# Cross-attention on one core: the third token group's softmax moves its subtraction and its row sums into ScalarE's exponentials

## The chip, the core and the metric

The kernel runs on one core of one Trainium2 chip. The time is the device time of one execution in microseconds (us), the median over the runs shown. A core has five engines that run side by side, each with its own in-order queue: TensorE (PE in the profile; its weight loads are PEld), VectorE (DVE), ScalarE (ACT), GpSimd (POOL) and SyncE (SP, which here only issues transfers). They wait for each other through semaphores.

## What is computed

A cross-attention layer with residual. 2 batches of 2048 tokens with 640 channels ask 154 context rows of 1024 channels; there are 20 heads of 32 channels. The context is cut in two halves of 77 rows, "text" and "ip", with key and value weights of their own, and each half has a softmax of its own; the two results are added.

```python
q = split_heads(hidden_states @ Wq.T)
k, v = split_heads(text @ Wk.T), split_heads(text @ Wv.T)
k_ip, v_ip = split_heads(ip @ Wk_ip.T), split_heads(ip @ Wv_ip.T)
def attend(q, k, v):
    scores = einsum('bhsd,bhld->bhsl', q, k) / sqrt(32)
    return einsum('bhsl,bhld->bhsd', softmax(scores, axis=-1), v)
out = merge_heads(attend(q, k, v)) + merge_heads(attend(q, k_ip, v_ip))
return out @ Wo.T + bo + hidden_states
```

The softmax takes each row's maximum away before the exponential, and divides by the row's sum. Everything is in fp32.

## The kernel before, in words

**Units.** The work is cut into 20 units. A unit is one batch, one chunk of 128 channels (4 heads) and one block of 1024 tokens. The 128 tokens that stand on the partitions at a time are a tile, so a unit has 8 tiles; they are taken in three groups, `GROUPS = ((0, 3), (3, 3), (6, 2))`: groups 0 and 1 have three tiles each, group 2 (the "third group") two. A tile has 4 heads x 2 halves = 8 softmax rows of 77 per partition, so groups 0 and 1 have 24 rows (1848 elements) per partition and group 2 has 16 rows (1232 elements).

**The steps of one group**, each a word in a schedule, with the unit's number behind the dot and the group's number in front of it (E2.5 is step E of group 2 in unit 5):

- R (`scores`, L223): TensorE computes the scores of the group into four PSUM banks, one per head.
- K (`take`, L235): ScalarE copies the four banks into the buffer `pb` in SBUF, one copy per bank. Only then may TensorE use these banks again.
- M (`maxima`, L261): VectorE takes the maximum of each row.
- S (`subtract`, L275): GpSimd subtracts it, in place.
- E (`exponential`, L281): ScalarE takes the exponential of the whole group in one instruction, in place.
- D (`sums`, L288 and L290): VectorE sums each row, and takes the reciprocal.
- N (`normalise`, L295): GpSimd multiplies by it.
- T (`transpose`, L302): VectorE transposes 32 x 32 blocks in place.

After two units comes A (`attend`, L311): TensorE multiplies the transposed weights with the values, and CA (`take_attention`, L334 and L338) copies the result out on ScalarE. Beside this stand, per chunk, the projections of keys and values (k and v, L132; ck and cv are their copies on ScalarE, L673 and L675), the query projections (q, L191; cq is the scaled copy on ScalarE, L201), and, from unit 10 on, the output projection of the first batch (words m, o, cm, co and G; L457 to L508), written as seven products in place of eight. The output projection of the second batch comes last, after the last attend (words V, X, F, Y; L815 to L835).

**What sets the order.** The list `SCHEDULE` is written out by hand, and `emit` turns each word into instructions in that order. Each engine's queue follows the order of its own words. For ScalarE the words are K, E, cq, ck, cv and CA; for VectorE M, D, T and the sums of the output projection; for GpSimd S, N and G. Two halves of four PSUM banks serve everything on TensorE: "@0" and "@1" behind an R or an A name the half, "@4" behind a q or a k the single bank. So a K, cq, cv, ck or CA that is late on ScalarE holds a bank (or the queries) that TensorE needs for a later word.

The change touches `exponential_of` (L244, which the kernel before never calls, since `DIRECT` is empty), `maxima` (L257), `sums` (L285), `normalise` (L293) and the dispatch in `emit` (L650 to L663). The schedule itself stays as it is.

Of the kernel before, what the change touches and what calls it, by code (L numbers as in the profile page):

```python
# [20 lines left out]
def kernel(  # L21
# [25 lines left out]
    nc = tc.nc  # L47
    P = 128
    NC = C // P
    NCC = CC // P  # L50
    G = P // D
# [7 lines left out]
    L = TEXT  # L59
# [1 line left out]
    NK = (2 * L + D - 1) // D  # L61
    LP = NK * D
    SCALE = 1.0 / float(D) ** 0.5
    DIRECT = {}
    NP = B * NC
    NU = NP * SUB
    OPEN = 4
# [4 lines left out]
    small = ctx.enter_context(tc.tile_pool(name="small", bufs=4))  # L72
# [137 lines left out]
    def keys_of(u, s):  # L210
        return pb_of(u, s)[:, :, :, : 2 * L]

    def rows_of(u, s):
        return keys_of(u, s).rearrange("p n g (t l) -> p (n g) t l", l=L)

    def scores(u, s, ps):

        _, b, c, _ = step_of(u)
        first, n = GROUPS[s]
        for t in range(n):  # L220
            h, st = divmod(first + t, TB // P)
            for g in range(G):
                nc.tensor.matmul(  # L223
                    ps[g][:, ts(t, 2 * L)],
                    qTs[(u, h)][g * D : (g + 1) * D, ts(st, P)],
                    kT[g * D : (g + 1) * D, c, b].rearrange("p t l -> p (t l)"),
                    start=True,
                    stop=True,
                )

    def take(u, s, ps):

        n = GROUPS[s][1]
        for g in range(G):
            nc.scalar.copy(  # L235
                keys_of(u, s)[:, :, g], ps[g][:, : n * 2 * L].rearrange("p (n l) -> p n l", n=n)
            )
# [3 lines left out]
    def rows_in(ps, n):  # L241
        return ps[:, : n * 2 * L].rearrange("p (n t l) -> p n t l", n=n, t=2)

    def exponential_of(u, s, ps):  # L244

        n = GROUPS[s][1]
        for g in range(G):
            for t in range(n):
                for x in range(2):
                    nc.scalar.activation(  # L250
                        rows_of(u, s)[:, t * G + g, x],
                        rows_in(ps[g], n)[:, t, x],
                        AF.Exp,
                        bias=maxs[(u, s)][:, t * G + g, x : x + 1],
                    )

    def maxima(u, s, ps=None):  # L257
        n = GROUPS[s][1] * G
        mx = small.tile([P, n, 2], F32, tag=f"mx{n}", name=f"mx_{u}_{s}")
        if ps is None:  # L260
            nc.vector.tensor_reduce(mx, rows_of(u, s), AX.X, ALU.max)  # L261
# [21 lines left out]
    rdens = {}  # L283

    def sums(u, s):  # L285
        n = GROUPS[s][1] * G
        den = small.tile([P, n, 2], F32, tag=f"den{n}", name=f"den_{u}_{s}")
        nc.vector.tensor_reduce(den, rows_of(u, s), AX.X, ALU.add)  # L288
        rden = small.tile([P, n, 2], F32, tag=f"rden{n}", name=f"rden_{u}_{s}")
        nc.vector.reciprocal(rden, den)  # L290
        rdens[(u, s)] = rden

    def normalise(u, s):  # L293
        n = GROUPS[s][1] * G
        nc.gpsimd.tensor_tensor(  # L295
            rows_of(u, s), rows_of(u, s), rdens[(u, s)].unsqueeze(3).to_broadcast([P, n, 2, L]), ALU.mult
        )

    def transpose(u, s):
# [4 lines left out]
    def attend(q, pa):  # L304

        zones = pb[:, ds(q % 2, SUB)].rearrange("p z n g (k s) -> p (z n) g k s", k=NK)
        for k in range(NK):
            for r in range(G):
                rows = slice(r * D, (r + 1) * D)
                for g in range(G):  # L310
                    nc.tensor.matmul(  # L311
                        pa[r][g * D : (g + 1) * D, :],
                        v4s[q % 2][rows, g, k, :],
                        zones[rows, :, g, k, :],
                        start=(k == 0),
                        stop=(k == NK - 1),
                    )
# [10 lines left out]
    def take_attention(q, pa):  # L328
        b, c = divmod(q, NC)
        rows = rows_of_attention(b, c).rearrange("p i (n r s) -> p r i n s", n=NT // NH, r=G)  # L330
        for r in range(G):
            tokens = pa[r].rearrange("p (i n s) -> p i n s", i=NHB, n=NT // NH)
            if q % 2 == 0:
                nc.scalar.copy(rows[:, r], tokens)  # L334
                continue

            for sub in range(SUB):
                nc.scalar.copy(rows[:, r, ts(sub, NH)], tokens[:, ts(1 - sub, NH)])  # L338
# [204 lines left out]
    for t in range(2):  # L543

        ps = halves[t][G - 2 + t]
# [76 lines left out]
    def emit(word):  # L622
        name, _, where = word.partition("@")
        k, *args = name.split(".")
        x, y = (*(int(a) for a in args if a.isdigit()), None, None)[:2]
        i = int(k[1:]) if k[1:].isdigit() else None
        if k[0] == "R":
            at[name] = halves[int(where)]
            scores(x, i, at[name])
        elif k == "A":  # L630
            at[name] = halves[int(where)]
            attend(x, at[name])
        elif k == "CA":
            take_attention(x, at[f"A.{x}"])
        elif k == "SQ":
            square_v(x)
        elif k == "VS":
            spread_v(x, y)
        elif k == "LX":
            load_block(x, y)  # L640
        elif k == "LQ":
            load_wq(x)
        elif k == "LK":
            load_w(x)
        elif k == "LO":
            load_wo()
        elif k == "LF":
            for part in PARTS:
                fetch(0, part)
        elif k[0] in "KMSEDNT":  # L650
            ps = at[f"R{i}.{x}"]
            if k[0] == "K":
                take(x, i, ps)
            elif k[0] in "ME":
                direct = (x, i) in DIRECT
                if k[0] == "M":
                    maxima(x, i, ps if direct else None)
                elif direct:
                    exponential_of(x, i, ps)
                else:  # L660
                    exponential(x, i)
            else:
                dict(S=subtract, D=sums, N=normalise, T=transpose)[k[0]](x, i)  # L663
        elif k == "q":
            at[name] = banks[int(where)]
            queries(x, y, at[name])
        elif k == "cq":
            take_queries(x, y, at[name[1:]])
        elif k in ("k", "v"):
            at[name] = banks[int(where)]  # L670
            project_kv(4 * x + 2 * (k == "v") + y, at[name])
        elif k == "ck":
            nc.scalar.copy(kT[:, x, :, y, :], keys_in(at[name[1:]]))  # L673
        elif k == "cv":
            nc.scalar.copy(vT[:, :, ds(y * L, L)], keys_in(at[name[1:]]))  # L675
        elif k in ("o", "p"):
            at[name] = banks[int(where)]
            last_chunk(at[name], int(k == "p"), x, range(NC - (k == "p")))
        elif k == "co":
            store_last(at[name[1:]], 0, x)  # L680
        elif k[0] == "m":
            at[name] = banks[int(where)] if where else at[f"m{JOINS[i]}.{x}"]
            product(i, 0, x, at[name])
        elif k[:2] == "cm":
            take_product(int(k[2:]), 0, x, at[name[1:]])
        elif k[0] == "W":
            sum_w(i)
        elif k[0] == "G":
            sum_t(i, 0, x)
        else:  # L690
            finish(k, args, where)
# [152 lines left out]
    for word in SCHEDULE:  # L844
        emit(word)
# [32 lines left out]
```

## Time and profile before

| | |
|---|---|
| median of 2 runs | 509.73 us (509.55 to 509.91) |
| the profiled execution: first to last instruction (span) | 509.3 us, mean granted TensorE clock 0.990 |
| busy of TensorE / VectorE / GpSimd / ScalarE | 496.4 / 431.5 / 414.3 / 242.8 us |
| chain that ended last, by engine | PE 69%, DVE 9%, DMA 8%, POOL 8%, ACT 2% |

How to read it. A group's row gives the line, the engine and the operation, the tiles written and read, the shape, the count, then the busy time, the mean duration of one in ns, and the idle time of the engine in front of these instructions with what ended it ("<-POOL pb L275" means: a result of line 275 on GpSimd). In a timeline the first two columns are the start and the length in us; instructions of one kind that follow each other are merged ("x4"). The busy time of TensorE counts pipelined matmuls by modelled ends, so the gaps between starts say more than the busy share. The clock in the table is the share of the TensorE clock that was granted.

### The profile page before, as it was taken

What the parts mean: (1) busy time and instruction counts of PE and PEld (TensorE: products, weight loads), DVE (VectorE), ACT (ScalarE), POOL (GpSimd) and SP (SyncE); (2) the same over time, 40 slices, a digit from 0 to 9 for tenths busy, and PEclk for the clock granted to TensorE, in tenths of its full rate; (3) what the DMA queues carried; (4) which work ended last, traced back from release to release, by engine and by line L of the source; (5) the groups of instructions that cost most, each with busy time, mean ns of one, the idle gap of its engine ahead of it and who ended that gap; (6) DMA issues with size and microseconds to landing.
All of it is one profiled execution on the core that took longest, in us unless ns stands there. A gap on an engine that the chain in (4) does not pass through costs nothing.

```text
span 509.3 us, 9862 instructions
## 1 busy us (share of the span) xinstructions
PE 496.4 (97%) x4114; PEld 292.1 (57%) x4114; DVE 431.5 (85%) x401; ACT 242.8 (48%) x423; POOL 414.3 (81%) x176
## 2 busy tenths in 40 slices
PE   9999999999989999999999999996999999999996
PEld 5657557557458556446655565553666576444442
DVE  0078989989987989977995999799299999999986
ACT  1266657577566567654636544663466453100000
POOL 0078999999997979988998899799399999468750
PEclk9999999999999999999999999997999999999999
DMA  8994050502441554577444724534914022310017
GB/s 272 357 287 134 16 136 11 142 3 71 129 148 42 157 192 141 200 238 250 146 134 146 242 62 155 210 106 134 322 30 124 27 82 64 125 62 1 21 62 268
DMA packets 67468, 69.34 MB, mean 136 GB/s; under 512 B 5472, under 2 KB 47200, under 8 KB 67424
## 3 DMA queue, kind: packets, MB, share of 16 engines
q1 hardware_dynamic: 66704, 68.00, 42.5%
q8 instruction: 32, 0.52, 0.4%
q10 hardware_dynamic: 720, 0.72, 0.4%
q14 instruction: 12, 0.10, 0.1%
HBM read 54.94 MB, written 10.49 MB: 128 GB/s over the span
## 4 chain that ended last, share of the span: by engine, by line
PE 69%; DVE 9%; DMA 8%; POOL 8%; ACT 2%; SPq 2%; issue 1%; DVEq 0%; POOLq 0%
PE bank L191 22%; PE bank L835 11%; PE bank L477 8%; PE bank L223 8%; PE bank L311 6%; PE bank L132 6%; POOL pb L275 5%; PE bank L457 4%; DMA x<-in_x_dram 3%; DVE pb L302 3%; POOL pb L295 3%; PE bank L487 2%; DVE mx L261 2%; DVE den L288 2%; DMA wo_ct<-in_L_xattn_Wo_dram 2%; DMA aT<-in_L_xattn_Wk_ip_dram 2%
## 5 line engine op out<-in xcount | busy, mean ns | idle before, releaser
L275 POOL TENSOR_TENSOR pb<-pb,mx 128x1848 f32<-128x1848 f32 (+1 forms) x60 | 175.6, 2946 | 42.4 <-DVE mx L261 42.3
L295 POOL TENSOR_TENSOR pb<-pb,rden 128x1848 f32<-128x1848 f32 (+1 forms) x60 | 175.6, 2948 | 15.4 <-DVE rden L290 15.1
L191 PE MATMUL bank<-x,wq 128*128 128x512 f32 x400 | 182.5, 606 | 4.8 <-DMA x<-in_x_dram 4.5
L261 DVE TENSOR_REDUCE mx<-pb 128x24 f32<-128x1848 f32 (+1 forms) x60 | 109.3, 1837 | 34.4 <-ACT pb L235 34.4
L191 PEld LDWEIGHTS bank<-x,wq 128*128 128x128 f32 x400 | 75.0, 193 | 92.8 <-issue 82.8
L235 ACT COPY pb<-bank 128x462 f32<-128x462 f32 (+1 forms) x240 | 101.9, 534 | 54.2 <-PE bank L223 53.6
L281 ACT ACTIVATE pb<-pb 128x1848 f32<-128x1848 f32 (+1 forms) x60 | 94.9, 1583 | 68.0 <-POOL pb L275 67.8
L288 DVE TENSOR_REDUCE den<-pb 128x24 f32<-128x1848 f32 (+1 forms) x60 | 110.2, 1836 | 16.3 <-ACT pb L281 16.3
L302 DVE STREAM_TRANSPOSE pb<-pb 128x1920 f32<-128x1920 f32 (+1 forms) x60 | 114.6, 1924 | 0.9 <-POOL pb L295 0.9
L223 PEld LDWEIGHTS bank<-kT,qT 32*128 32x128 f32 x1280 | 47.1, 185 | 27.6 <-issue 20.2
L223 PE MATMUL bank<-kT,qT 32*128 32x154 f32 x1280 | 58.8, 307 | 1.6 <-issue 1.3
L311 PE MATMUL bank<-pb,v 32*32 32x512 f32 x1600 | 55.5, 597 | 0.7 <-ACT pb L235 0.7
L132 PE MATMUL bank<-wo_ct,aT 128*128 128x154 f32 x320 | 46.8, 301 | 0.4 <-DMA aT<-in_L_xattn_Wk_ip_dram 0.3
L132 PEld LDWEIGHTS bank<-wo_ct,aT 128*128 128x128 f32 x320 | 44.3, 192 | 4.7 <-issue 3.5
L311 PEld LDWEIGHTS bank<-pb,v 32*32 32x32 f32 x1600 | 29.8, 103 | 22.3 <-issue 10.1
L201 ACT ACTIVATE qT<-bank 128x512 f32<-128x512 f32 x40 | 23.5, 599 | 29.3 <-PE bank L191 29.2
L457 PE MATMUL bank<-aT,wo_ct 128*128 128x512 f32 x80 | 36.3, 595 | 0.0
L477 PE MATMUL bank<-aT,wo_ct 128*128 128x256 f32 x128 | 32.3, 386 | 0.0
L477 PEld LDWEIGHTS bank<-aT,wo_ct 128*128 128x128 f32 x128 | 23.6, 190 | 7.6 <-issue 4.4
L502 DVE SCALAR_TENSOR_TENSOR acc<-bank,bo_sb,acc 128x256 f32<-128x256 f32 x32 | 13.6, 466 | 14.9 <-PE bank L487 14.8
L457 PEld LDWEIGHTS bank<-aT,wo_ct 128*128 128x128 f32 x80 | 15.0, 190 | 16.8 <-issue 16.4
L781 DVE TENSOR_TENSOR x<-x,bank 128x512 f32<-128x512 f32 x36 | 23.1, 678 | 1.0 <-PE bank L835 0.9
(71 smaller groups left out, 343.0 us busy)
## 6 DMA issues: line engine op xcount, KB each, us to landing
x<-in_x_dram SPq DMA_DIRECT2D x20, 1280.0 KB, 8.4
out_dram<-acc SPq DMA_DIRECT2D x20, 256.0 KB, 2.6
x<-in_x_dram SPq DMA_DIRECT2D x18, 256.0 KB, 5.4
acc<-in_x_dram SPq DMA_DIRECT2D x16, 256.0 KB, 3.7
out_dram<-x SPq DMA_DIRECT2D x15, 256.0 KB, 2.3
v<-vS SPq DMA_DIRECT2D x160, 20.0 KB, 2.6
wq<-in_L_xattn_Wq_dram SPq DMA_DIRECT2D x9, 320.0 KB, 5.3
aT<-in_L_xattn_Wk_dram SPq DMA_DIRECT2D x5, 512.0 KB, 4.5
```

Of the source, the lines that this page charges most:

```text
L132: nc.tensor.matmul(keys_in(out), loaded[n][:, k, :], cT[:, k, :, t, :], start=(k == 0), stop=(k == NCC - 1))
L191: nc.tensor.matmul(pq, wqs[q % 3][:, k, :], xs[place_of(u, h)][:, k, :], start=(k == 0), stop=(k == NC - 1),)
L223: nc.tensor.matmul(ps[g][:, ts(t, 2 * L)], qTs[(u, h)][g * D : (g + 1) * D, ts(st, P)], kT[g * D : (g + 1) * D, c, b].rearrange("p t l -> ...
L235: nc.scalar.copy(keys_of(u, s)[:, :, g], ps[g][:, : n * 2 * L].rearrange("p (n l) -> p n l", n=n))
L261: nc.vector.tensor_reduce(mx, rows_of(u, s), AX.X, ALU.max)
L275: nc.gpsimd.tensor_tensor(rows_of(u, s), rows_of(u, s), maxs[(u, s)].unsqueeze(3).to_broadcast([P, n, 2, L]), ALU.subtract)
L281: nc.scalar.activation(e, e, AF.Exp)
L288: nc.vector.tensor_reduce(den, rows_of(u, s), AX.X, ALU.add)
L295: nc.gpsimd.tensor_tensor(rows_of(u, s), rows_of(u, s), rdens[(u, s)].unsqueeze(3).to_broadcast([P, n, 2, L]), ALU.mult)
L302: nc.vector.transpose(p, p)
L311: nc.tensor.matmul(pa[r][g * D : (g + 1) * D, :], v4s[q % 2][rows, g, k, :], zones[rows, :, g, k, :], start=(k == 0), stop=(k == NK - 1),)
L477: nc.tensor.matmul(part, w_of[m][:, kp, op], t_of(m, b, i)[:, kp], start=(op == kp == 0 and m in (1, 2, 5)), stop=(op == 1 and kp == 1 and ...
```

## The change

For group 2 of every unit (20 times): the maximum is written negated; the subtraction on GpSimd is left out; the one exponential over 1232 elements becomes 16 exponentials over one row of 77 each, with the row's negated maximum as the activation's bias (one value per partition) and the row's sum written by the activation itself (`accum_out`); the row sum on VectorE is left out, and only the reciprocal stays. Groups 0 and 1 are unchanged. The words of the schedule keep their places; S of group 2 emits nothing.

```diff
-    DIRECT = {}
+    MODES = {2: "ra"}
...
+    def mode(u, s):
+        return MODES.get(s, "")
+
+    def exponential_by_rows(u, s, ps):
         n = GROUPS[s][1]
+        if "a" in mode(u, s):
+            dens[(u, s)] = small.tile([P, n * G, 2], F32, tag=f"den{n * G}", name=f"den_{u}_{s}")
         for g in range(G):
             for t in range(n):
                 for x in range(2):
+                    row = rows_of(u, s)[:, t * G + g, x]
+                    more = {"accum_out": dens[(u, s)][:, t * G + g, x : x + 1]} if "a" in mode(u, s) else {}
                     nc.scalar.activation(
-                        rows_of(u, s)[:, t * G + g, x],
-                        rows_in(ps[g], n)[:, t, x],
+                        row,
+                        rows_in(ps[g], n)[:, t, x] if "p" in mode(u, s) else row,
                         AF.Exp,
                         bias=maxs[(u, s)][:, t * G + g, x : x + 1],
+                        **more,
                     )
...
-            nc.vector.tensor_reduce(mx, rows_of(u, s), AX.X, ALU.max)
+            nc.vector.tensor_reduce(mx, rows_of(u, s), AX.X, ALU.max, negate="r" in mode(u, s))
...
     def sums(u, s):
         n = GROUPS[s][1] * G
-        den = small.tile([P, n, 2], F32, tag=f"den{n}", name=f"den_{u}_{s}")
-        nc.vector.tensor_reduce(den, rows_of(u, s), AX.X, ALU.add)
+        if (u, s) in dens:
+            den = dens[(u, s)]
+        else:
+            den = small.tile([P, n, 2], F32, tag=f"den{n}", name=f"den_{u}_{s}")
+            (nc.gpsimd if "g" in mode(u, s) else nc.vector).tensor_reduce(den, rows_of(u, s), AX.X, ALU.add)
...
+            elif k[0] == "S" and ("p" in mode(x, i) or "r" in mode(x, i)):
+                pass
...
-                elif direct:
-                    exponential_of(x, i, ps)
+                elif "r" in mode(x, i) or "p" in mode(x, i):
+                    exponential_by_rows(x, i, ps)
                 else:
                     exponential(x, i)
```

The letters "p", "g" and "d" of the new modes are not used by this change, which has "r" and "a" alone.

More of the change, by code (lines that the diff above doesn't have):

```diff
@@ L249, in exponential_of @@
                 for x in range(2):
+                    row = rows_of(u, s)[:, t * G + g, x]
+                    more = {"accum_out": dens[(u, s)][:, t * G + g, x : x + 1]} if "a" in mode(u, s) else {}
                     nc.scalar.activation(
-                        rows_of(u, s)[:, t * G + g, x],
-                        rows_in(ps[g], n)[:, t, x],
+                        row,
+                        rows_in(ps[g], n)[:, t, x] if "p" in mode(u, s) else row,
                         AF.Exp,
                         bias=maxs[(u, s)][:, t * G + g, x : x + 1],
+                        **more,
                     )
+    dens = {}
     def maxima(u, s, ps=None):
@@ L286, in sums @@
         n = GROUPS[s][1] * G
-        den = small.tile([P, n, 2], F32, tag=f"den{n}", name=f"den_{u}_{s}")
-        nc.vector.tensor_reduce(den, rows_of(u, s), AX.X, ALU.add)
+        if (u, s) in dens:
[3 more added lines that the diff above has]
+            (nc.gpsimd if "g" in mode(u, s) else nc.vector).tensor_reduce(den, rows_of(u, s), AX.X, ALU.add)
+        if "d" in mode(u, s):
+            rdens[(u, s)] = den
+            return
         rden = small.tile([P, n, 2], F32, tag=f"rden{n}", name=f"rden_{u}_{s}")
@@ L295, in normalise @@
         nc.gpsimd.tensor_tensor(
-            rows_of(u, s), rows_of(u, s), rdens[(u, s)].unsqueeze(3).to_broadcast([P, n, 2, L]), ALU.mult
+            rows_of(u, s), rows_of(u, s), rdens[(u, s)].unsqueeze(3).to_broadcast([P, n, 2, L]), ALU.divide if 'd' in mode(u, s) else ALU.mult
         )
@@ L652, in emit @@
             if k[0] == "K":
-                take(x, i, ps)
+                if "p" not in mode(x, i):
+                    take(x, i, ps)
+            elif k[0] == "S" and ("p" in mode(x, i) or "r" in mode(x, i)):
+                pass
             elif k[0] in "ME":
-                direct = (x, i) in DIRECT
                 if k[0] == "M":
-                    maxima(x, i, ps if direct else None)
-                elif direct:
-                    exponential_of(x, i, ps)
+                    maxima(x, i, ps if "p" in mode(x, i) else None)
+                elif "r" in mode(x, i) or "p" in mode(x, i):
+                    exponential_by_rows(x, i, ps)
                 else:
```

1 line of the change is left out of this document (removed).

## The prediction, as put on record before the changed kernel ran

> **What bounds the kernel now.** I read the busy times first, then the busy time by stretch, then the waits of TensorE and ScalarE, and last the timelines around single exponentials.
>
> ```profile
> PE 496.4 (97%) x4114; PEld 292.1 (57%) x4114; DVE 431.5 (85%) x401; ACT 242.8 (48%) x423; POOL 414.3 (81%) x176
> ```
>
> ```profile
> 20.00:112.00 92.00, 91.43 (x903) 58.11 (x901) 78.38 (x59) 57.81 (x102) 79.71 (x28) 1.00 0.44 124
> 112.00:210.00 98.00, 96.47 (x941) 60.37 (x934) 89.42 (x69) 64.13 (x118) 90.85 (x32) 0.98 0.45 139
> 210.00:410.00 200.00, 194.75 (x1790) 115.31 (x1791) 171.32 (x146) 105.30 (x178) 178.91 (x73) 0.98 0.47 151
> 410.00:445.00 35.00, 34.66 (x293) 21.43 (x292) 34.03 (x46) 11.38 (x21) 28.11 (x17) 1.00 0.26 84
> ```
>
> ```profile
> PE bank L191 <- DMA x<-in_x_dram: 4.5, 2, 3.8
> PE bank L223 <- issue: 1.3, 1, 1.3
> PE bank L538 <- DVE pb L536: 1.1, 1, 1.1
> PE bank L311 <- ACT pb L235: 0.7, 1, 0.7
> PE bank L835 <- ACT aT L338: 0.3, 1, 0.3
> PE bank L223 <- ACT kT L548: 0.3, 1, 0.3
> ```
>
> In the stretches the columns after the length are PE, PEld, DVE, ACT and POOL. TensorE is busy in 417.3 of the 425 us in which softmax work runs (20 to 445), and it waits for a transfer (4.5), at an unnamed place (1.3), and for other engines in crumbs (0.7, 0.3, 0.3). GpSimd and VectorE are nearly full too, but hardly ever does TensorE wait for them. So taking work from them can win at most 1.3 + 0.7 + 0.3 + 0.3 = 2.6 us. ScalarE is half idle, and that suggests room; but its idle time is waiting inside an in-order queue whose results TensorE takes almost at once. What counts is how long TensorE can do without them.
>
> **The change part by part.** The rows of the instructions concerned (busy us, mean ns, then idle in front):
>
> ```profile
> L235 ACT COPY pb<-bank 128x462 f32<-128x462 f32 x160 | 75.9, 579 | 40.5 <-PE bank L223 40.5
> L281 ACT ACTIVATE pb<-pb 128x1848 f32<-128x1848 f32 x40 | 70.3, 1757 | 57.7 <-POOL pb L275 57.7
> L275 POOL TENSOR_TENSOR pb<-pb,mx 128x1232 f32<-128x1232 f32 x20 | 45.1, 2257 | 3.6 <-DVE mx L261 3.6
> L261 DVE TENSOR_REDUCE mx<-pb 128x16 f32<-128x1232 f32 x20 | 28.2, 1408 | 3.6 <-ACT pb L235 3.5
> L288 DVE TENSOR_REDUCE den<-pb 128x16 f32<-128x1232 f32 x20 | 27.9, 1396 | 0.3 <-ACT pb L281 0.3
> L281 ACT ACTIVATE pb<-pb 128x1232 f32<-128x1232 f32 x20 | 24.7, 1237 | 10.4 <-POOL pb L275 10.1
> L548 ACT COPY kT<-bank 128x77 f32<-128x77 f32 x4 | 0.7, 227 | 3.8 <-PE bank L132 3.8
> ```
>
> 1. Removed: 20 subtractions on GpSimd (45.1 us) and 20 sums on VectorE (27.9 us). TensorE's own stream hides both; by the bound above they are worth 0 to 2.6 us. I take 0. The last unit's softmax (the end of the stretch 410 to 445) could use the 2.26 us on GpSimd, but TensorE is busy there in 34.66 of 35 us.
>
> 2. The negated maximum: no row shows one. The bounds are the plain maximum's 1408 ns, and that plus another pass as long (20 x 1.4 = 28 us on VectorE, with GpSimd's subtraction no longer behind it). The instruction and shape stay the same, so I take 0.
>
> 3. Added: 16 exponentials of 77 elements in place of one of 1232, in 20 blocks, so 320. No row shows an exponential with a bias per partition and a written sum. The two exponential rows give (1757 - 1237) / 616 = 0.844 ns per element and 1237 - 1232 x 0.844 = 197 ns fixed, so 197 + 65 = 262 ns for a lone one of 77. Lower end: ScalarE overlaps plain copies.
>
> ```profile
> 20.33 0.35 ACT L548 COPY kT<-bank 128x77 f32<-128x77 f32 x2 [1.51 <-PE bank L132]
> ```
>
> Two copies of the same size take 0.35 us together at 227 ns each, so one starts 0.12 us after the other; 16 x 0.125 = 2.0 us per block. Upper end: no overlap, and the written sum is an instruction of its own as long as such a copy: 262 + 227 = 489 ns, 7.8 us per block. I take 0.30 us each, near the middle and a little over the lone 262 ns: the bias and the sum should cost something, overlap gives some back. A block is then 16 x 0.30 = 4.80 us in place of 1.24, so 3.56 us more. The Trainium skill, page "ScalarE: Activation LUTs", section "What ACT_TABLE_LOAD costs", says that a bias by pointer adds about 93 ns and that activations back to back overlap by about 93 ns: an estimate from it is 280 + 64 - 93 = 251 ns, without the sum. By that a block would be 4.0 us, and the sum below would give 520 in place of 530.
>
> 4. The wait for the subtraction goes. Block 14 alone waits 5.31 us for it (row below), the others (10.4 - 5.3) / 19 = 0.27 each. What is late next: the block follows what stands in front of it in ScalarE's queue. So ScalarE comes out 3.56 - 0.27 = 3.3 us later at each block but the 14th. In the built order some row exponentials carry a wait for an earlier copy of their bank, also on ScalarE; it has long ended, and three such waits a block, at the 17 ns of a semaphore row below, are 0.05 us.
>
> ```profile
> L281 ACTq EVENT_SEMAPHORE  x4: 17/17/17, 263.9 to 320.6; - x4
> ```
>
> 5. What is queued behind the block on ScalarE, and who waits for it. Each time it is a cq, cv, ck, K or CA, that TensorE needs for banks or queries. I went through all 20 blocks in ScalarE's timeline and added, until the first result that TensorE lacks, ScalarE's idle time and the margin between that result and TensorE's use: that is the block's cover. Block 0 (first), block 1 (tight), block 10 (free) and block 18 (last that loses), ScalarE's rows and then TensorE's:
>
> ```profile
> 38.16 1.24 ACT L281 ACTIVATE pb<-pb 128x1232 f32<-128x1232 f32 x1
> 40.08 0.29 ACT L675 COPY vT<-bank 128x154 f32<-128x154 f32 x1 [0.69 <-PE bank L132]
> ...
> 54.00 1.23 ACT L281 ACTIVATE pb<-pb 128x1232 f32<-128x1232 f32 x1 [0.27 <-POOL pb L275]
> 55.79 0.60 ACT L201 ACTIVATE qT<-bank 128x512 f32<-128x512 f32 x1 [0.56 <-PE bank L191]
> ...
> 231.39 1.23 ACT L281 ACTIVATE pb<-pb 128x1232 f32<-128x1232 f32 x1 [0.68 <-POOL pb L275]
> 236.40 1.89 ACT L235 COPY pb<-bank 128x462 f32<-128x462 f32 x4 [3.77 <-PE bank L223]
> ...
> 307.56 1.23 ACT L281 ACTIVATE pb<-pb 128x1232 f32<-128x1232 f32 x1 [5.31 <-POOL pb L275]
> ...
> 405.19 1.24 ACT L281 ACTIVATE pb<-pb 128x1232 f32<-128x1232 f32 x1 [0.46 <-POOL pb L275]
> 406.33 0.58 ACT L201 ACTIVATE qT<-bank 128x512 f32<-128x512 f32 x1
> ```
>
> ```profile
> 39.97 1.85 PE L223 MATMUL bank<-kT,qT 32*128 32x154 f32 x48
> ...
> 55.69 1.80 PE L223 MATMUL bank<-kT,qT 32*128 32x154 f32 x40
> ...
> 256.87 0.74 PE bank L223 x16
> ...
> 408.64 1.07 PE L223 MATMUL bank<-kT,qT 32*128 32x154 f32 x24
> ```
>
> Block 0: 0.69 idle, and the second 24 of the 48 score matmuls (at about 40.9) need the bank that the copy of 40.08 freed at 40.37: cover 1.3 with the overlap of neighbours (0.1). Block 1: 0.56 idle; 16 score matmuls take 0.74 to 0.77 us, so the other 24 of the 40 start at 56.46 and need the queries that end at 55.79 + 0.60 = 56.39; cover 0.7. Block 10: 3.77 idle and nothing urgent; cover 3.9. Block 18: the queries end at 406.91, the matmuls at 408.64 need them; cover 1.7. All covers (us), blocks 0 to 9: 1.3, 0.7, 0.2, 1.0, 1.9, 2.2, 2.0, 3.1, 2.5, 2.4; blocks 10 to 19: 3.9, 5.3, 1.1, 5.0, block 14 by its own 5.3 of wait, 3.2, 2.6, 3.5, 1.7, 4.7.
>
> TensorE loses 3.3 less the cover where that is positive: blocks 0 to 9 lose 2.0 + 2.6 + 3.1 + 2.3 + 1.4 + 1.1 + 1.3 + 0.2 + 0.8 + 0.9 = 15.7; the others 2.2 + 0.1 + 0.7 + 1.6 = 4.6 (blocks 12, 15, 16, 18). Sum 20.3 us. The first half loses most because there TensorE alternates short pieces (scores, projections of keys and values) over the same banks; later the output projection stands between.
>
> 6. The reciprocal on VectorE stays and waits for the block's end. The sum had waited only 0.3 us in 20 for its exponential, so VectorE came after it; now the reciprocal may come 3.3 - 1.4 = 1.9 us later than the old one, with maxima and transposes of other units queued behind. TensorE needs transposes only at the ten attends; I take 0, and up to 10 x 1.9 = 19 us as the far end. Normalise on GpSimd waits with it, with 2.26 us per unit freed. No transfer is added or moved in SP's queue; those that wait for TensorE shift with it.
>
> The profiled execution has a span of 509.3; the runs have 509.55 and 509.91 (median 509.73), 0.4 above it. 509.3 + 20.3 + 0.4 = 530.0.
>
> **The rivals.** *It hides (not slower).* If the row exponentials overlap like copies, a block takes 2.0 us, the shift is 0.5, only block 2 loses (0.3), and the 2.6 us may come back: 507 to 510. At 0.20 us each the shift is 1.7 and the loss 0.4 + 1.0 + 1.5 + 0.7 + 0.6 = 4.2: 514. It decides at about 0.25 us each (loss 10.5, 520). For it speaks the copies' 0.12 us; against it, that a written sum must wait for the last element.
>
> *Each sum is a serial step.* At 0.49 us each a block is 7.84, the shift 6.3, and 19 blocks lose 71: 581. At 0.40 the shift is 4.9 and the loss 45: 555. For it speaks the fixed 197 ns, three times the work of 77 elements; against it the overlap that all plain ScalarE rows show. The Trainium skill, page "VectorE: DVE Perf Modes", section "Two Vector instructions with no wait between them", says of VectorE that an instruction which also writes its accumulator is two, the main one and an accumulator read; no row here shows whether ScalarE does so.
>
> *The clock drops as well.* After TensorE's one long wait its next ten matmuls took 7.34 us; ten at full clock take 4.56:
>
> ```profile
> 350.82 7.34 PE L191 MATMUL bank<-x,wq 128*128 128x512 f32 x10 [3.85 <-DMA x<-in_x_dram]
> 57.42 4.56 PE L191 MATMUL bank<-x,wq 128*128 128x512 f32 x10
> ```
>
> That is 2.8 us more per stall of about 3.9 us. My longest stall is 3.1 us, so I count none; at 0.40 us each, four blocks (0, 1, 2, 3) come near and would add up to 11 to that rival.
>
> *Faster by over 2%* would need 10 us, and the bound is 2.6.
>
> **How the numbers follow.** Forecast (0.25 to 0.40 us each): 0.53, with its own range 520 to 555 and 530 as its value. It hides (below 0.25 us, 507 to 520): 0.26. Serial sums (above 0.40, 555 to 585, the clock's share in it): 0.20. Faster: 0.01. About 2% (10.2 us) is what a measurement of this kernel can tell from no change: slower 0.73, same 0.26, faster 0.01. The range 512 to 572 leaves out about 0.1 of the first rival and 0.09 of the second.
>
> **What would show each step.** The new rows: 320 exponentials of 77 elements, and the length of a block from its first to its last (4.8 us expected; 2.0 or 7.8 are the rivals). TensorE's waits should name ScalarE (queries, value and score copies), mostly before 210, at the blocks with short cover, and block 10 and 11 should cost nothing. TensorE's idle time should grow by about 20 us, GpSimd's and VectorE's busy time fall by 45 and 28 us. Blocks of 4.8 us with a time near 510 would refute the covers; TensorE waiting for transposes would refute point 6; a maximum longer than 1.4 us would refute point 2; granted clock well under 0.99 would show the third rival.

## The result, and the profile after

| | before | after |
|---|---|---|
| median of 2 runs | 509.73 us | 554.44 us (553.77 to 555.11) |
| ratio, with its 95% interval | | 1.0878 (1.0845 to 1.0910) |
| profiled execution: span, mean granted clock | 509.3 us, 0.990 | 553.2 us, 0.969 |

The change costs 44.7 us, a little more than twice the 20.3 forecast. Some executions of a kernel come out slow, over 1.5% above its fastest; the medians and ratios here and below leave them out. The same views as before, now of the changed kernel. First the page's busy times:

```profile
PE 513.3 (93%) x4114; PEld 305.0 (55%) x4114; DVE 405.6 (73%) x381; ACT 324.0 (59%) x1043; POOL 371.0 (67%) x156
```

GpSimd lost 43.3 us of work and VectorE 25.9, close to the 45.1 and 27.9 that were taken out. TensorE lost nothing to do, yet it is "busy" 16.9 us longer: a first sign that its clock matters. The stretches (length, PE, PEld, DVE, ACT, POOL, granted clock, DMA share, GB/s; the last runs to the end of the program):

```profile
20.00:112.00 92.00, 82.04 (x669) 55.13 (x667) 54.90 (x41) 60.66 (x201) 54.99 (x18) 0.91 0.40 113
112.00:210.00 98.00, 89.31 (x848) 55.87 (x845) 74.91 (x57) 73.29 (x237) 69.10 (x24) 0.95 0.30 83
210.00:410.00 200.00, 191.07 (x1797) 112.72 (x1796) 155.38 (x132) 139.34 (x435) 153.12 (x60) 0.99 0.52 171
410.00:553.00 143.00, 131.97 (x755) 70.61 (x753) 120.24 (x153) 47.60 (x172) 92.92 (x50) 0.99 0.23 76
```

Compare the count of matmuls with the same stretch before: 669 against 903 from 20 to 112, and 848 against 941 from 112 to 210. Most of the loss is in the first half, as the covers said; and there the clock fell from 1.00 and 0.98 to 0.91 and 0.95. TensorE's waits (total us, times, longest):

```profile
PE bank L223 <- ACT qT L201: 14.1, 8, 3.0
PE bank L223 <- ACT vT L693: 7.7, 3, 3.7
...
PE bank L132 <- ACT aT L354: 1.9, 1, 1.9
PE bank L327 <- ACT qT L201: 1.8, 1, 1.8
PE bank L327 <- issue: 1.3, 1, 1.3
PE bank L554 <- DVE pb L552: 1.1, 1, 1.1
PE bank L223 <- ACT pb L235: 1.0, 1, 1.0
```

Before, ScalarE stood in this view with 0.7 + 0.3 + 0.3 = 1.3 us. Now its rows alone here make 14.1 + 7.7 + 1.9 + 1.8 + 1.0 = 26.5 us: queries (L201), value copies (L693), attention copies (L354), score copies (L235). The 1.1 us for VectorE is the row of before (L538 there, L554 here). No row names a softmax transpose, but the 1.3 us put down to "issue" is one: that attend (L327) starts as VectorE's transposes end, at 436.08 + 5.62 = 441.70.

```profile
436.08 5.62 DVE L318 STREAM_TRANSPOSE pb<-pb 128x1280 f32<-128x1280 f32 x3
```

```profile
441.81 5.66 PE L327 MATMUL bank<-pb,v 32*32 32x512 f32 x160 [1.27 <-issue]
```

The instructions of the third group, one group per shape:

```profile
L257 ACT ACTIVATE pb<-pb,mx 128x77 f32<-128x77 f32 x320 | 109.7, 356 | 1.3 <-DVE mx L271 1.3
...
L257 ACT ACTIVATION_READ_ACCUMULATOR pb<-pb,mx 128x1 f32 x320 | 63.0, 197 | 0.0
...
L271 DVE TENSOR_REDUCE mx<-pb 128x16 f32<-128x1232 f32 x20 | 28.2, 1410 | 9.6 <-ACT pb L235 9.6
...
L306 DVE RECIPROCAL rden<-den 128x16 f32<-128x16 f32 x20 | 4.7, 238 | 41.2 <-ACT pb L257 41.2
```

The written sum is an instruction of its own: 320 exponentials come with 320 accumulator reads. How the two interleave is seen in ScalarE's timeline at block 1:

```profile
60.35 0.35 ACT L257 ACTIVATE pb<-pb,mx 128x77 f32<-128x77 f32 x1
60.60 0.19 ACT L257 ACTIVATION_READ_ACCUMULATOR pb<-pb,mx 128x1 f32 x1
60.70 0.34 ACT L257 ACTIVATE pb<-pb,mx 128x77 f32<-128x77 f32 x1
...
65.73 0.19 ACT L257 ACTIVATION_READ_ACCUMULATOR pb<-pb,mx 128x1 f32 x1
65.83 0.58 ACT L201 ACTIVATE qT<-bank 128x512 f32<-128x512 f32 x1
```

The read starts 0.25 us after its exponential, the next exponential about 0.09 after the read: 0.343 us per row over the 16. The block runs from 60.35 to 65.92, so it takes 5.5 us with its last overlap taken off, where 4.8 was forecast. The queries' copy starts at 65.83. TensorE meanwhile:

```profile
62.41 1.06 PE L223 MATMUL bank<-kT,qT 32*128 32x154 f32 x22
66.46 1.05 PE L223 MATMUL bank<-kT,qT 32*128 32x154 f32 x18 [2.98 <-ACT qT L201]
67.43 6.26 PE L191 MATMUL bank<-x,wq 128*128 128x512 f32 x10
```

The score matmuls halt for the queries that end at 65.83 + 0.58 = 66.41, as the prediction had said of block 1. And the ten matmuls after that take 6.26 us; before they took 4.56.

**The 43.9 us of span in three parts.** Both traces hold TensorE's 4114 matmuls in the same order, so their starts can be paired one by one. Where the distance between two neighbouring starts differs by more than 0.5 us, it is a stall: 28.5 us in all. The growth inside stretches where either trace's granted clock is 0.50 is the clock's: 10.8. The many small differences make 4.6, and where these come from stays open. A cross-check of the clock's part: if the clock is either 1 or 0.5, a mean of 0.969 over 553.2 means 2 x 0.031 x 553.2 = 34 us at half clock, and 0.990 over 509.3 means 10; 24 more at half speed cost at most 12.

### The profile page after: what moved, and what is told of

Its sections match the earlier page's. It is cut to its first block, busy times and chain, and to the rows that moved or that the text cites. A ratio compares the mean times of both kernels' runs of the same rounds, so it can differ in the third digit from the quotient of the medians.

```text
span 553.2 us, 10427 instructions
## 1 busy us (share of the span) xinstructions
PE 513.3 (93%) x4114; PEld 305.0 (55%) x4114; DVE 405.6 (73%) x381; ACT 324.0 (59%) x1043; POOL 371.0 (67%) x156
## 3 DMA queue, kind: packets, MB, share of 16 engines
q1 hardware_dynamic: 66704, 68.00, 39.2%
## 4 chain that ended last, share of the span: by engine, by line
PE 47%; ACT 24%; DVE 15%; DMA 6%; POOL 6%; issue 1%; SPq 1%; DVEq 0%; POOLq 0%
ACT pb L257 15%; PE bank L191 14%; PE bank L853 8%; PE bank L223 7%; PE bank L132 6%; PE bank L493 5%; ACT pb L291 4%; PE bank L327 4%; DVE mx L271 4%; DVE den L301 4%; POOL pb L285 4%; DVE pb L318 3%; DMA x<-in_x_dram 3%; ACT pb L235 3%; PE bank L473 2%; POOL pb L311 2%
## 5 line engine op out<-in xcount | busy, mean ns | idle before, releaser
L285 POOL TENSOR_TENSOR pb<-pb,mx 128x1848 f32<-128x1848 f32 x40 | 131.2, 3286 | 81.9 <-DVE mx L271 81.9
L235 ACT COPY pb<-bank 128x462 f32<-128x462 f32 (+1 forms) x240 | 101.3, 526 | 45.9 <-PE bank L223 45.8
L257 ACT ACTIVATE pb<-pb,mx 128x77 f32<-128x77 f32 x320 | 109.7, 356 | 1.3 <-DVE mx L271 1.3
L301 DVE TENSOR_REDUCE den<-pb 128x24 f32<-128x1848 f32 x40 | 82.4, 2061 | 24.8 <-ACT pb L291 24.5
L291 ACT ACTIVATE pb<-pb 128x1848 f32<-128x1848 f32 x40 | 70.3, 1760 | 34.9 <-POOL pb L285 34.9
L223 PE MATMUL bank<-kT,qT 32*128 32x154 f32 x1280 | 66.2, 321 | 24.3 <-ACT qT L201 14.1
L223 PEld LDWEIGHTS bank<-kT,qT 32*128 32x128 f32 x1280 | 52.1, 194 | 52.6 <-ACT qT L201 19.2
L257 ACT ACTIVATION_READ_ACCUMULATOR pb<-pb,mx 128x1 f32 x320 | 63.0, 197 | 0.0
L327 PE MATMUL bank<-pb,v 32*32 32x512 f32 x1600 | 55.7, 597 | 3.1 <-ACT qT L201 1.8
L132 PE MATMUL bank<-wo_ct,aT 128*128 128x154 f32 x320 | 52.0, 323 | 2.1 <-ACT aT L354 1.9
L132 PEld LDWEIGHTS bank<-wo_ct,aT 128*128 128x128 f32 x320 | 49.5, 212 | 6.7 <-issue 2.7
L306 DVE RECIPROCAL rden<-den 128x24 f32<-128x24 f32 (+1 forms) x60 | 16.7, 281 | 42.6 <-ACT pb L257 41.2
L327 PEld LDWEIGHTS bank<-pb,v 32*32 32x32 f32 x1600 | 30.9, 103 | 24.0 <-issue 10.6
L201 ACT ACTIVATE qT<-bank 128x512 f32<-128x512 f32 x40 | 23.4, 596 | 26.2 <-PE bank L191 26.1
```

Of the source, the lines that this page charges most:

```text
L132: nc.tensor.matmul(keys_in(out), loaded[n][:, k, :], cT[:, k, :, t, :], start=(k == 0), stop=(k == NCC - 1))
L223: nc.tensor.matmul(ps[g][:, ts(t, 2 * L)], qTs[(u, h)][g * D : (g + 1) * D, ts(st, P)], kT[g * D : (g + 1) * D, c, b].rearrange("p t l -> ...
L235: nc.scalar.copy(keys_of(u, s)[:, :, g], ps[g][:, : n * 2 * L].rearrange("p (n l) -> p n l", n=n))
L257: nc.scalar.activation(row, rows_in(ps[g], n)[:, t, x] if "p" in mode(u, s) else row, AF.Exp, bias=maxs[(u, s)][:, t * G + g, x : x + 1], ...
L285: nc.gpsimd.tensor_tensor(rows_of(u, s), rows_of(u, s), maxs[(u, s)].unsqueeze(3).to_broadcast([P, n, 2, L]), ALU.subtract)
L291: nc.scalar.activation(e, e, AF.Exp)
```

## The experiments

Two theories stood after this. **Queue:** only the time that the block occupies ScalarE counts; each block's excess beyond its cover stalls TensorE, and longer stalls bring a slower clock on top. **Kind:** something peculiar to the new instructions (their sums, the bias, VectorE's negated maximum, the reciprocal that waits) holds others up beside the occupation. Differences in us are between the medians of the kernel and of the one before on the same chip; for the change that is the 44.7 above. Where 509.25 is the median before, its five runs spread from 508.4 to 513.7, so those two differences are good to some 4 us.

| kernel | block, us | median (before), us | ratio (95%) |
|---|---|---|---|
| relief alone | 1.24 | 510.54 (510.94) | 0.998 (0.996 to 1.001) |
| plain rows | 2.6 | 515.71 (510.94) | 1.009 (1.006 to 1.011) |
| rows with sum, no bias | 4.0 | 530.11 (509.25) | 1.037 (1.029 to 1.046) |
| rows with bias, no sum | 4.1 | 532.01 (510.94) | 1.039 (1.034 to 1.045) |
| before + 14 copies | 5.3 | 555.34 (511.31) | 1.085 (1.079 to 1.091) |
| before + 30 copies | 10.2 | 653.83 (510.94) | 1.280 (1.276 to 1.284) |
| change in 7 covered units | 5.5 | 514.87 (511.31) | 1.007 (1.003 to 1.010) |
| change in 9 tight units | 5.5 | 543.11 (511.31) | 1.063 (1.055 to 1.072) |
| change, 7 blocks moved later, 1 earlier | 5.5 | 550.46 (511.31) | 1.076 (1.071 to 1.082) |
| change, 7 blocks split, 1 moved earlier | 5.5 | 534.48 (509.25) | 1.045 (1.036 to 1.054) |

### The relief alone

Subtraction and row sums of the third group go; nothing is added. Its rows are then divided by their maxima in place of their sums.

```diff
     def subtract(u, s):
+        if s == 2:
+            return
...
     def sums(u, s):
...
+        if s == 2:
+            den = maxs[(u, s)]
+        else:
...
```

> The kernel before, with group 2's subtraction on GpSimd and its sum on VectorE left out and nothing put in their place (these rows are not shifted by their maximum, and are divided by the maximum in place of the sum). Theory: TensorE hides both, so at most 2.6 us are won: 507 to 510. Rival (GpSimd and VectorE limit the softmax stretches): 73 us of work less, 495 to 503.

0.4 us less, between 2.2 less and 0.5 more by the ratio's interval. Its busy time from 20 to 445 us in the stretches' sum:

```profile
sum 425.00, PE 417.46 PEld 255.84 DVE 344.60 ACT 236.26 POOL 333.89; mean PE 104.37 PEld 63.96 DVE 86.15 ACT 59.07 POOL 83.47
```

and the same of the kernel before:

```profile
sum 425.00, PE 417.31 PEld 255.23 DVE 373.15 ACT 238.62 POOL 377.58; mean PE 104.33 PEld 63.81 DVE 93.29 ACT 59.66 POOL 94.40
```

44 us fewer on GpSimd, 29 fewer on VectorE, and TensorE goes on as before. What the change takes away is worth nothing here.

### Plain rows

The kernel before, subtraction and sum kept, but the third group's exponential cut into 16 plain ones.

```diff
+        if s == 2:
+            ...
+                        row = rows_of(u, s)[:, t * G + g, x]
+                        nc.scalar.activation(row, row, AF.Exp)
+            return
```

> The kernel before, with group 2's exponential cut into 16 rows of 77, without bias and without written sum; subtraction and sum stay where they were. Theory: plain activations start about 0.13 us apart, a block is 2.1 us, shift 0.85, only the two tightest blocks lose (0.15 + 0.65): 510 to 512. Rival (the number of ScalarE instructions costs, whatever they take): 520 or more.

```profile
38.95 2.62 ACT L285 ACTIVATE pb<-pb 128x77 f32<-128x77 f32 x16
```

16 take 2.62 us; one lasts 0.26, so they start (2.62 - 0.26) / 15 = 0.157 apart, more than the copies' 0.12. The shift is 2.62 - 1.24 = 1.38. By the prediction's covers the blocks 1, 2, 3, 12 and 0 then lose 0.7 + 1.2 + 0.4 + 0.3 + 0.1 = 2.7 us; measured 4.8. The run's forecast of 510 to 512 was missed: a row was taken at 0.13 us, and 2 us more came that the covers do not give.

### The bias without the sum, and the sum without the bias

```diff
-    MODES = {2: "ra"}
+    MODES = {2: "r"}
```

> Row exponentials with the negated maximum as bias, but no written sum; VectorE sums the rows again. Theory (ScalarE's added time beyond each block's cover, plus half-clock windows): in the changed kernel one exponential and its accumulator read start 0.34 us after the pair before, of which 0.25 until the read; without the read 0.25 us per row remains, a block of 4.0 us, shift 2.5, loss 10.5 us by the covers plus 2 to 5 for the clock: 521 to 526. Rival (the late softmax chain on VectorE and GpSimd costs the time): VectorE has its 28 us of sums back, so no better than the changed kernel, 550 to 560.

```profile
39.30 4.11 ACT L257 ACTIVATE pb<-pb,mx 128x77 f32<-128x77 f32 x16
```

The profiled execution has a span of 536.4, longer than the median of the runs, so only durations are taken from it. (4.11 - 0.36) / 15 = 0.250 us per row: the bias costs 0.093 over a plain row. The Trainium skill, page "ScalarE: Activation LUTs", section "What ACT_TABLE_LOAD costs", names about 93 ns for a pointer operand; this pair of runs agrees. The run's forecast of 521 to 526 was missed: 21.1 us are lost, where the covers gave 10.5 and the clock was put at 2 to 5.

The other one keeps GpSimd's subtraction and has `accum_out` but no bias:

```diff
-    MODES = {2: "ra"}
+    MODES = {2: "a"}
...
-                        bias=maxs[(u, s)][:, t * G + g, x : x + 1],
```

> Row exponentials with the written sum but without bias; GpSimd subtracts as before the change, VectorE's sum is left out. By the runs so far a plain row takes 0.16 us and a bias adds 0.09; if the accumulator read adds another 0.09, a row takes 0.25 us and a block 4.0 to 4.1 us, as with the bias alone. Theory (ScalarE's added time beyond the covers, plus the clock): the same 10 to 13 us by the covers, a little more since the wait for the subtraction stays, 526 to 536. Rival (the read alone is what the change pays for): 545 or more; rival (the read is free): 513 to 517.

```profile
38.34 0.27 ACT L257 ACTIVATE pb<-pb 128x77 f32<-128x77 f32 x1
38.51 0.19 ACT L257 ACTIVATION_READ_ACCUMULATOR pb<-pb 128x1 f32 x1
...
42.10 0.25 ACT L257 ACTIVATE pb<-pb 128x77 f32<-128x77 f32 x1
```

From the first to the 16th start (42.10 - 38.34) / 15 = 0.251 us: the sum costs the same 0.093 as the bias. Together 0.157 + 0.093 + 0.093 = 0.343, the row of the change. And two kernels whose blocks are equally long for different reasons (4.1 and 4.0 us) lose about the same, 21.1 and 20.9 us (the second between 15 and 23 by the ratio's interval). Paired with the kernel before, the trace of the second has 13.6 us of stalls; its shift of 4.02 - 1.24 = 2.8 gives 14.0 by the covers. That speaks for the queue; the next one decides.

### The kernel before with copies behind each block

No row exponential, no bias, no sum on ScalarE, nothing relieved: only copies in a tile that nobody reads.

```diff
                     exponential(x, i)
+                    if i == 2:
+                        for _ in range(14):
+                            nc.scalar.copy(fill[1], fill[0])
```

> The kernel before, with 30 copies of 96 elements (to a tile that nobody reads) behind each exponential of group 2 on ScalarE; subtraction, sum and exponential as before. That adds about 4.3 us of ScalarE time per block, as much as the row exponentials did, and nothing else. Theory (occupied ScalarE alone makes the loss): 35 us by the covers and 8 to 14 for the clock, 550 to 560, as the changed kernel. Rival (half of the loss comes from the bias, the sum or the later reciprocal): 525 to 540.

The dose came out too high:

```profile
39.04 9.04 ACT L666 COPY fill<-fill 128x96 f32<-128x96 f32 x30
```

That is 0.30 us per copy, with no overlap. That they all write one tile is the likely reason; no run here tests it apart. As a test of the change's size it says little, but it gives the far end: 142.9 us lost. With 14 copies:

> As the run with 30 copies, with 14: each copy there started 0.30 us after the one before (it waits for it, since it writes the same tile), so 14 add 4.2 us per block, the dose that was meant. Theory (occupied ScalarE alone makes the loss): 34 us by the covers and 8 to 12 for the clock, 550 to 556, as the changed kernel. Rival (half of the loss comes from the bias, the sum or the later reciprocal): 525 to 540.

ScalarE's timeline at block 0, and two of TensorE's waits, both with 14 copies:

```profile
38.75 1.24 ACT L283 ACTIVATE pb<-pb 128x1232 f32<-128x1232 f32 x1
39.88 4.20 ACT L666 COPY fill<-fill 128x96 f32<-128x96 f32 x14
```

```profile
PE bank L225 <- ACT qT L203: 15.1, 9, 2.8
PE bank L225 <- ACT vT L680: 7.2, 3, 3.5
```

The copies end at 44.08, the exponential at 39.99: copies alone that hold ScalarE 4.1 us longer lose 44.0 us, where the change with a shift of 4.0 loses 44.7, and TensorE's two longest rows are those of the change (14.1 and 7.7 there). Paired with the kernel before in the same way, this trace has 28.9 us of stalls, 11.7 of clock and 4.2 of small differences, where the change has 28.5, 10.8 and 4.6. "Kind" falls: the time of a queue is enough.

From 14 to 30 copies each block grows by 4.84 us, 20 blocks by 97, and the time by 98.5. It looks as if each further microsecond were paid 20 times, but that is a coincidence: paired with each other, the two traces differ by 64.6 us of stalls, 29.4 of clock and 4.8 of small differences.

### The change in some units only

```diff
-        return MODES.get(s, "")
+        return MODES.get(s, "") if u in (10, 11, 13, 14, 15, 17, 19) else ""
```

> The change in seven units alone (10, 11, 13, 14, 15, 17, 19), those whose blocks had covers of 3.2 us or more (14: its own wait). Theory: a block of 5.5 us comes out 4.0 us later, losing 0.1 + 0.8 + 0.5 us there: 510 to 514. Rival (each changed block costs the same): 7/20 of 44 us, 524 to 528.

3.6 us lost, where the covers at the measured shift give 0.1 + 0.8 + 0.5 = 1.4; the time is just above the forecast of 510 to 514. Of TensorE's rows none names the queries' copy any more; what grew against the kernel before (1.3 in the first row there) or is new is small. The last row is a wait of an attend for a transpose, and the 1.3 us in front of another attend is the one seen in the change:

```profile
PE bank L223 <- issue: 2.6, 2, 1.4
PE bank L327 <- issue: 1.3, 1, 1.3
...
PE bank L327 <- DVE pb L318: 1.0, 1, 1.0
```

The same with the nine units 0 to 6, 12 and 18:

> The change in nine units alone (0 to 6, 12 and 18), with covers of 0.2 to 2.2 us. Theory: 24 us by the covers and 8 to 12 for the clock, 540 to 548. Rival (each changed block costs the same): 9/20 of 44 us, 528 to 532.

```profile
PE bank L223 <- ACT qT L201: 10.2, 5, 3.0
```

31.8 us lost, as forecast. The covers, read off the kernel before, thus separate seven blocks that cost 0.5 us each from nine that cost 3.5 each. The four that are in neither (7, 8, 9, 16) lose 0.9 + 1.5 + 1.6 + 0.8 = 4.8 by the covers at the measured shift; 3.6 + 31.8 + 4.8 = 40.2 of the 44.7.

### Eight blocks moved behind what TensorE waits for

If covers are the matter, a block should cost little behind the urgent copies. In the schedule E2 of units 0, 1, 2, 3, 5, 12, 16 and 18 goes to a later place (16: an earlier one), with D2 and N2 where they follow; for instance:

```diff
-v.0.0@1 cv.0.1 E2.0 D2.0 R0.1@1 cv.0.0
+v.0.0@1 cv.0.1 R0.1@1 cv.0.0
...
-K0.1 k.1.1@4 K1.1 M0.1 k.1.0@6 LK.9 ck.1.1 M1.1 S0.1
+K0.1 k.1.1@4 K1.1 E2.0 M0.1 k.1.0@6 LK.9 ck.1.1 M1.1 D2.0 S0.1
```

> The changed kernel, with the row exponentials of units 0, 1, 2, 3, 5, 12, 16 and 18 moved in the written schedule, behind the copies that TensorE waits for (the reciprocal, and in units 1 and 5 the normalise, go behind them); every instruction is the same. Theory: these eight blocks then lose about 2 us in all, the others 9 to 10, and the clock 2 to 4: 520 to 528. Rival (the added work costs wherever it stands): 545 to 556.

39.2 us lost in place of 44.7: only 5.5 came back, and the forecast for this run (520 to 528) was missed. TensorE's waits show why:

```profile
PE bank L327 <- issue: 10.1, 4, 3.7
...
PE bank L132 <- ACT aT L354: 3.5, 1, 3.5
PE bank L191 <- ACT kT L694: 3.4, 1, 3.4
```

and VectorE's timeline in front of one of those attends (L327), then TensorE's:

```profile
76.30 2.18 DVE L318 STREAM_TRANSPOSE pb<-pb 128x1920 f32<-128x1920 f32 x1 [1.73 <-POOL pb L311]
```

```profile
78.58 8.26 PE L327 MATMUL bank<-pb,v 32*32 32x512 f32 x160 [3.69 <-issue]
```

The transpose ends at 78.48, the attend begins at 78.58: this wait, put down to "issue", ends with the transpose. The other three of these attends, at 120.70, 167.56 and 437.22, likewise start 0.1 us behind the end of a transpose. The later block hands its sums on later; reciprocal, GpSimd's normalise and VectorE's transpose slide back until the attend waits for them, and attention and key copies (L354, L694) are now the late ones on ScalarE. A block of 5.5 us has two deadlines, the copies behind it and the attend that needs its own result, and at these places the room between them was too small for the whole.

### Seven blocks split

So the block is cut: for units 0, 1, 2, 3, 5, 12 and 18 eight rows stay, and eight come behind the urgent copy (a new word e2). Unit 16's block goes to an earlier place, where ScalarE had been idle; the words D2 of units 0, 2, 3 and 5 and N2 of unit 5 follow their blocks. The instructions are those of the change.

```diff
+    def exponential_by_rows(u, s, ps, part=0):
...
-        for g in range(G):
+        for g in range(G) if u not in SPLIT else range(2 * part, 2 * part + 2):
...
-K1.1 M0.1 k.1.0@6 LK.9 ck.1.1 M1.1
+K1.1 M0.1 k.1.0@6 LK.9 ck.1.1 e2.0 M1.1
```

> The changed kernel, with the row exponentials of units 0, 1, 2, 3, 5, 12 and 18 cut in two halves of eight: the first stays in its place, the second stands behind the copies that TensorE waits for; unit 16's stand earlier, where ScalarE idled 9.7 us. Theory (each block has a cover ahead, the next copies, and one behind, the attend that waits for the transposes; moving whole blocks back spent the second one): these eight units lose about 5 us in place of 21, and most half-clock windows go: 525 to 535. Rival (the later half makes the transposes as late as moving the whole block did): 545 to 556.

```profile
PE bank L223 <- ACT qT L201: 5.1, 5, 2.5
...
PE bank L223 <- ACT vT L700: 2.9, 2, 1.6
```

25.2 us lost (18 to 28 by the ratio's interval) in place of 44.7, with a granted clock of 0.984 in place of 0.969: about 20 us come back by order alone. Paired with the kernel before, the trace has 15.2 us of stalls and 2.3 of clock, where the change has 28.5 and 10.8. Queries and values together wait 8.0 us where they waited 21.8. Still slower than the kernel before, and it could hardly be otherwise: the relief alone, with nothing added, gained 0.4 us.

## Why the prediction was too low, point by point

Two steps failed: the price of a row in point 3 (0.30 us, measured 0.343), worth 10.4 us, and the clock, counted as none and worth 10.8. The path, ScalarE's queue with a cover for each block, was right. The measured 554.44 lies at the end of the range 520 to 555, but by luck: that end stood for rows of 0.40 us at full clock.

**Points 1 and 2 hold.** The relief is worth 0.4 us (2.2 less to 0.5 more). The negated maximum takes 1410 ns, the plain one took 1408.

**Point 3 failed in its size.** "I take 0.30 us each, near the middle and a little over the lone 262 ns" should have been 0.343. The parts: a plain row of 77 starts 0.157 us after the one before (not 0.125 as the copies), the bias adds 0.093, the sum 0.093. The prediction let overlap cancel most of bias and sum. They do not: each adds its 0.093 on top of a row that already overlaps. It had named the right ingredient, a sum that is an instruction of its own, only as the far end; here it lasts 197 ns, of which 93 show. The Trainium skill's page "VectorE: DVE Perf Modes", section "Two Vector instructions with no wait between them", says of VectorE that an accumulator output is a second instruction; the new rows show it for ScalarE.

**Points 4 and 5 hold, with the right shift.** A block of 5.5 gives a shift of 5.5 - 1.24 - 0.27 = 4.0 in place of 3.3. The same covers then give 2.7 + 3.3 + 3.8 + 3.0 + 2.1 + 1.8 + 2.0 + 0.9 + 1.5 + 1.6 = 22.7 in blocks 0 to 9 and 0.1 + 2.9 + 0.8 + 1.4 + 0.5 + 2.3 = 8.0 in the others: 30.7. In the trace, 27.3 of the 28.5 us of stalls stand behind these blocks; the attend's wait for its transposes is 1.3 more, and two others cancel. One by one (0: no stall over 0.5 us):

| block | 0 | 1 | 2 | 3 | 4 | 5 | 6 | 7 |
|---|---|---|---|---|---|---|---|---|
| by the cover | 2.7 | 3.3 | 3.8 | 3.0 | 2.1 | 1.8 | 2.0 | 0.9 |
| stall in the trace | 3.0 | 3.3 | 3.8 | 3.3 | 1.7 | 1.4 | 0.8 | 0.7 |

| block | 8 | 9 | 10 | 12 | 15 | 16 | 17 | 18 |
|---|---|---|---|---|---|---|---|---|
| by the cover | 1.5 | 1.6 | 0.1 | 2.9 | 0.8 | 1.4 | 0.5 | 2.3 |
| stall in the trace | 1.8 | 1.6 | 0 | 0.7 | 0 | 1.7 | 1.0 | 2.5 |

The covers of blocks 12 and 6 were read too short (2.9 and 2.0 us by the cover, 0.7 and 0.8 in the trace); blocks 10 and 11 cost nothing, as forecast. So 0.043 us per row is 0.7 us per block and 10.4 us in the sum by the covers. The loss is steep there: between a block of 4.0 and one of 5.5 the time rises by 24 us.

**The third rival was part of the answer.** "My longest stall is 3.1 us, so I count none" failed: the clock's part is 10.8 us. Its threshold was taken from one long wait (3.85 us), and much shorter ones do it. Block 0 and a place behind an attend, in TensorE's timeline after:

```profile
44.49 1.92 PE L223 MATMUL bank<-kT,qT 32*128 32x154 f32 x22 [2.68 <-ACT vT L693]
46.33 6.63 PE L132 MATMUL bank<-wo_ct,aT 128*128 128x154 f32 x32
...
138.32 6.14 PE L132 MATMUL bank<-wo_ct,aT 128*128 128x154 f32 x32 [1.86 <-ACT aT L354]
```

and the granted clock (the third number from the right) in stretches behind these and behind the one of block 1:

```profile
44.00:50.80 6.80, 6.31 (x39) 6.00 (x40) 6.23 (x4) 3.94 (x11) 2.18 (x1) 0.50 0.16 45
67.90:71.20 3.30, 3.30 (x5) 1.35 (x4) 1.78 (x1) 1.49 (x4) 3.30 (x2) 0.50 0.13 29
139.60:142.80 3.20, 3.20 (x15) 3.20 (x14) 3.17 (x4) 2.32 (x6) 2.47 (x1) 0.50 0.00 0
```

A wait of 2.68 us, of 2.98, even of 1.86, and the clock stands at half for some 3.4 or 6.8 us; the 32 matmuls of 46.33 took 4.48 us before. The warning was there in the kernel before, at a place that the prediction passed over:

```profile
151.45 1.24 PE L223 MATMUL bank<-kT,qT 32*128 32x154 f32 x12 [1.32 <-issue]
152.62 5.66 PE L132 MATMUL bank<-wo_ct,aT 128*128 128x154 f32 x32
```

32 such matmuls in 5.66 us, behind a wait of 1.32. Yet waits of 1.31 us (ending at 158.92), 1.51 (242.04), 1.67 (415.43) and 1.77 (215.97) in the trace after are followed by full clock, so length alone does not settle it. The trace's record of the clock shows what else counts. The half-clock stretches begin at 43.95, 67.84, 95.15, 115.63, 139.52, 180.48, 385.28 and 450.14 us: always a whole number of steps of 3.413 us apart, and they last one or two such steps. All twelve traces show this step, each with an offset of its own. Two steps of this grid, the last before the fall at 139.52 and one that no fall followed (the number behind the length is TensorE's busy time):

```profile
136.11:139.52 3.41, 1.55 (x21) 1.32 (x14) 2.00 (x2) 3.41 (x9) 2.65 (x2) 1.00 0.02 5
412.59:416.00 3.41, 1.74 (x22) 1.26 (x20) 2.11 (x2) 3.41 (x20) 3.41 (x3) 1.00 0.16 36
```

Between 20 and 510 us TensorE was busy in 0.10 to 0.46 of each full-clock step that a fall followed, and in 0.51 or more of each of the others. So in this trace it matters how much idle time falls into one step, and not how long a single wait is. The border is not the same everywhere: in the kernel before, a step with 0.61 busy (148.24 to 151.65) was followed by a fall, and with 14 copies one with 0.94 (308.48 to 311.89). What else counts stays open.

The Trainium skill, page "TensorE: Matmul & The Clock Gate", section "Why this matters for your kernels", advises against idle gaps of more than about 3 us; here gaps under 3 us cost clock as well, and the measurement decides.

**Point 6 nearly holds in the change, but only because the block stood early.** The prediction took 0; one attend of the ten waits 1.3 us for its transposes, although the reciprocals waited 41.2 us in sum. With 14 copies one attend shows the same 1.3 us, though there no third-group reciprocal waits for the work added to its block. Where the change is made in the covered units alone, a second one waits 1.0 us; and with eight blocks moved that cover was gone, and four attends waited 10.1 us and a fifth 1.8.

The sum with the measured sizes: 20.3 + 10.4 (point 3) + 10.8 (clock) = 41.5 of the 43.9 between the two spans. Part of that agreement is luck: by the trace the blocks lose 27.3 us and not the 30.7 of the covers, the attend 1.3, the clock 10.8, and 4.6 lie in small differences that no term of the prediction holds. The rivals: "It hides" would have needed 0.25 us per row, and at that price the runs lost 21 us; "Each sum is a serial step" began at 0.40 us per row, so its mechanism (a read of its own) is there at a smaller price, and that its 555 at 0.40 us came out at 0.343 is a coincidence, since the clock came on top.

## What to carry to other kernels

An engine that is half idle is not free: in an in-order queue, count how long each block occupies the engine and subtract the time until the first result behind it that the bound engine lacks; the sum is steep, so a few hundredths of a microsecond per instruction, times 16 times 20, decide. Price a many-row form by its parts (start to start of a plain row, each pointer operand, each written sum as an instruction of its own), not by a lone instruction. And when a change makes the matrix engine wait, look for the shortest wait in the trace that a slower clock follows, not for the longest, and at how much idle time falls into one step of the clock's grid.

## What the runs showed of the hardware that was not expected

- ScalarE's written sum is a second instruction of about 0.19 us, of which 0.093 us shows between rows; a bias from memory shows the same 0.093. Plain exponentials of 77 elements start 0.157 us apart.
- Copies of 96 elements on ScalarE into one and the same tile start 0.30 us apart, where the two key copies of 77 elements into different places start 0.12 apart.
- TensorE's clock fell to half behind waits of 1.3 to 3.8 us, but not behind each of them. In each of the twelve traces the falls begin a whole number of steps of 3.413 us apart. In the trace after, up to 510 us, they last one or two steps, and each follows a step in which TensorE was busy 0.46 of the time or less.
